# Half-array matmuls for the last token tile and for the last 64 hidden units, another guest batch, and a new place for the transposes of norms

## The chip, the core and the metric

The kernel runs on one core of a Trainium2 chip. Its engines work side by side, each through its own queue in order: TensorE (PE) multiplies matrices into PSUM, VectorE (DVE) and ScalarE (ACT) read PSUM and write SBUF, GpSimd (POOL) works on SBUF and issues some transfers, SyncE (SP) issues the others. The metric is the device time of one execution in microseconds (us). All matmuls are float32; each matmul leaves two records in the trace, each transpose one. "x16" in a row of PE means 16 records.

## The reference, cut to what matters

For each of 16 batches, 100 query tokens of 256 channels attend to 361 context rows of 192 channels with 16 heads of 64 (cross-attention). Then all 1600 tokens pass a mixture of experts: a shared one, and one of seven that a router picks, each a SwiGLU with 704 hidden units.

```python
x = x + xattn(layernorm(x), ctx)         # q = x Wq; k, v = ctx Wkv; softmax(q k / 8) v; Wproj, bproj
h = layernorm(x)
shared = (silu(h @ sw1.T) * (h @ sw3.T)) @ sw2.T
p, e = top1(sigmoid(h @ router_w.T + routing_bias))
w = clip(0.5 + p, 0.5, 2.0)
x = x + 0.5 / w * shared + p / w * expert[e](h)
```

## The kernel before, in words

**Tiles.** The 1600 tokens make 13 tiles of 128; the last (tile 12) has only 64 rows. The 704 hidden units are five chunks of 128 and a rest of 64 (`HALF`). `GROUPS` puts the tiles into groups (0-2), (3-5), (6-8), (9-12).

**Attention.** The main loop walks over 32 steps (b, g): batch b, head half g = 0 or 1. Inside a step, `i` counts four pairs of heads. For each, PE makes the scores (`scores`, L645); DVE takes their maxima (L658), ACT the exponentials (L661); one pair later DVE transposes them (`turning`, L671 and L674). Between the scores PE works through `pairs`, products that other steps need: in (b, 1) the keys of batch b+1 and up to two of its three value products (both L568), in (b, 0) the value product that is left. At the end of a step with g = 0 come, on PE: the `fillers` (projections of finished token tiles, L744, and the router, L240), two query products (L544), and the attention values of batch b-1 (L717), in two halves, one for each of its steps. `moved` (L685 to L705) lies between a step and its L717: SP issues one transfer to `row`, eight to `aT` and two to `over`, POOL eight more to `aT`; then SP loads the context of a later batch (`cT`, L485) and copies guest rows (L587).

PE, ACT, DVE and SP run in the order in which the program is written here (L470). Every matmul product and every transpose takes one of eight PSUM banks in turn (`bank`, L120).

**Norms.** `normalised(g)` queues a group's layer norm in `norms` as parts: moments for each tile, the roots, one `normalise` (L188, DVE) for each tile, and a last part that puts the group's transposes (L208, PE, and the ACT copies to `xT`, L211) into `turns`. `part()` (L778) runs one such part; it is called three times in the loop over `i`, and once or twice behind it. `turns` is emptied at the start of each step with g = 0 (L818 to L820). With `keep`, the transposes also queue the group's router as a filler; its DVE work then goes through `norms` too.

**Guests.** The third key tile of a batch has only 105 of 128 keys, so it leaves 23 columns free. A guest batch has no third value product: five hosts compute its rows in their free columns, and a transfer (`host`, L582) puts them into `w2_sb`, which is not yet in use. Guests are batches 6 and 13, hosts 1 to 5 and 8 to 12.

**Shared expert.** `hidden` (L408) computes the hidden units of a group. The last chunk holds 64 units in its upper half; the lower half of `hT` and of `w2_sb` is set to zero, and `down` (L454) multiplies six chunks of 128 for each tile (L460), six matmuls of 256 columns, adds them into `acc` (L463, DVE) and stores the tile to `base_d`. `project` (L739) does eight matmuls of 256 columns for each tile, for the 64 rows of tile 12 too.

**Experts.** Sorted into tiles by expert, the tokens are gathered from `xn_d` and `base_d`. `turn` (L957) transposes a gathered tile (L960; ACT copies it to `xgT`, L962). A switch on the number of tiles (a load of `e_at`, L1027, and a branch) comes ahead of the loop over expert tiles (L969, L981).

Of the kernel before, what the change touches and what calls it, by code (L numbers as in the profile page):

```python
# [26 lines left out]
P = 128  # L27
# [12 lines left out]
HALF = I - NI * P  # L40
GROUPS = ((0, 1, 2), (3, 4, 5), (6, 7, 8), (9, 10, 11, 12))
FIRST, SECOND = (0, 1), (2, 3, 4, 5)
NS = (N - E) // P + E
NF = (N + P - 1) // P
WE = 2 * 2 * I + (NI + 1) * C
# [1 line left out]


FREE = P - JL
GUESTS = {6: (1, 2, 3, 4, 5), 13: (8, 9, 10, 11, 12)}  # L50
HOSTS = {host: (b, i) for b, hosts in GUESTS.items() for i, host in enumerate(hosts)}
HG = 8
WARM = 6
# [6 lines left out]
def xattn_moe(  # L60
# [18 lines left out]
    def rows(t):  # L79
        return P if t < NT - 1 else LAST  # L80
# [46 lines left out]
        nc.tensor.matmul(nothing[:, :P], ones, ones, start=True, stop=True)  # L127

    nc.gpsimd.memset(acc[LAST:, NT - 1, :], 0.0)
    nc.gpsimd.memset(w2_sb[: P - HALF, NI, :], 0.0)  # L130

    def load_x(g):
        full = [t for t in g if t < NT - 1]
# [85 lines left out]
    def load_shared(i):  # L219

        if i < 4:
            k, o = i // 2, ds(i % 2 * I, I)
            nc.sync.dma_start(w13_sb[:, k, o], w13[ts(k, P), o])
        elif i == 4:
            nc.sync.dma_start(w2_sb[:, :3, :], w2[: 3 * P].rearrange("(i p) c -> p i c", p=P))
        else:
            r = w2[3 * P : NI * P].rearrange("(i p) c -> p i c", p=P)
            nc.sync.dma_start(w2_sb[:, 3:NI, :], r)
            nc.sync.dma_start(w2_sb[P - HALF :, NI, :], w2[NI * P :])

    def router(tiles):

# [175 lines left out]
    def hidden(g, hT, sp, width=NB, same_table=0):  # L408


        n = sum(map(rows, g))

        nc.gpsimd.memset(hT[: P - HALF, NI, :n], 0.0)

        def product(to, at):
            for k in range(2):
                nc.tensor.matmul(  # L417
                    to[:, :n],
                    w13_sb[:, k, ds(at, P)],
                    xT[:, k, ds(g[0] * P, n)],  # L420
                    start=(k == 0),
                    stop=(k == 1),
                )

        def whole(i):
            pa, pb = bank(), bank()
            product(pa, i * P)
            product(pb, I + HALF + i * P)
            s = sp.tile([P, width], F32, name="s")
            if i < same_table:  # L430
                nc.scalar.activation(s[:, :n], pa[:, :n], AF.Tanh, scale=0.5)
                nc.vector.scalar_tensor_tensor(
                    s[:, :n], s[:, :n], 1.0, pa[:, :n], ALU.add, ALU.mult
                )
                nc.vector.scalar_tensor_tensor(
                    hT[:, i, :n], s[:, :n], 0.5, pb[:, :n], ALU.mult, ALU.mult
                )
                return
            nc.scalar.activation(s[:, :n], pa[:, :n], AF.Silu)
            nc.vector.tensor_tensor(hT[:, i, :n], pb[:, :n], s[:, :n], ALU.mult)  # L440

        def rest():

            pa = bank()
            product(pa, NI * P)
            s = sp.tile([P, width], F32, name="s")
            nc.scalar.activation(s[P - HALF :, :n], pa[:HALF, :n], AF.Silu)
            nc.vector.tensor_tensor(
                hT[P - HALF :, NI, :n], pa[P - HALF :, :n], s[P - HALF :, :n], ALU.mult
            )  # L450

        return [lambda i=i: whole(i) for i in range(NI)] + [rest]

    def down(g, hT):  # L454

        for i, t in enumerate(g):
            r = rows(t)
            y = bank()
            for c in range(NI + 1):
                nc.tensor.matmul(  # L460
                    y[:r, :C], hT[:, c, ds(i * P, r)], w2_sb[:, c, :], start=(c == 0), stop=(c == NI)
                )
            nc.vector.scalar_tensor_tensor(  # L463
                acc[:r, t, :], y[:r, :C], coef[:r, t : t + 1], acc[:r, t, :], ALU.mult, ALU.add
            )
            nc.sync.dma_start(base_d[t * P : t * P + r, :], acc[:r, t, :])


    with ExitStack() as attn:
# [10 lines left out]
        def load_ctx(b, parts=1):  # L480
            cT = ap2.tile([P, NR, NJ * P], F32, name="cT")
            of = ctxT[b].rearrange("p (k n) -> p k n", k=NR)
            for i in range(parts):
                k = ts(i, NR // parts)
                nc.sync.dma_start(cT[:, k], of[:, k])  # L485
            return cT

        wq_r = wq.rearrange("p (u k m) -> p u k m", u=NU, k=2)
# [250 lines left out]
        def project(t):  # L739
            r = rows(t)  # L740
            resT = resTs.pop(t)
            pp = bank()
            for c in range(NCH):
                nc.tensor.matmul(  # L744
                    pp[:r, :C], resT[:, c, QP : QP + r], wp_sb[:, c, :], start=(c == 0), stop=(c == NCH - 1)
                )
            nc.vector.tensor_tensor(acc[:r, t, :], pp[:r, :C], acc[:r, t, :], ALU.add)
# [66 lines left out]
        for s, (b, g) in enumerate(steps):  # L814

            if g == 0:  # L818
                while turns:
                    turns.popleft()()  # L820
                pairs = values_of.pop(b)
                if s == 0:
                    ask = lambda: qs.pop(0)() or (lambda: None)
                    pairs[1:] = [ask, ask] + pairs[1:]
                elif (b + 1) % QG == 0 and b + 1 < B:
                    qs = q_units((b + 1) // QG)
            elif b + 1 < B:
# [12 lines left out]
            tb = new_blocks()  # L840
            turning = None
            for i in range(n2):
                exponentials, then = scores(b, g * n2 + i)
                if puts:
                    puts.popleft()()
                exponentials()
                if turning:
                    turning(tb)
                    part()
                turning = then  # L850
                for _ in range(-(-len(pairs) // (n2 - i))):
# [24 lines left out]
        while norms or fillers or turns:  # L876
# [2 lines left out]
                turns.popleft()()  # L879
            if fillers:  # L880
                fillers.popleft()()
        down(GROUPS[0][:2], hT0)
        for at in range(NG):
            values(B - 1, at, *held.pop(0))
        down(GROUPS[0][2:], hT0[:, :, 2 * P :])
        finished(B - 1)
        while fillers:
            fillers.popleft()()
# [28 lines left out]
    def gather_into(to, of, k):  # L917
# [7 lines left out]
            oob_is_err=False,  # L925
        )

    with tc.tile_pool(name="hs", bufs=1) as hs:
        def run_hidden(g):
            n = sum(map(rows, g))  # L930
# [7 lines left out]
            one()  # L938
        hT = run_hidden(GROUPS[1])
        turn_last()  # L940
        down(GROUPS[1][:1], hT)
        for one in router(GROUPS[-1]):
            one()
        down(GROUPS[1][1:], hT[:, :, P:])
        fill = sort_tokens(hs)
        for k in range(NW):
            fetch(k)
# [9 lines left out]
    def turn(k):  # L957
        tr = bank()
        for j in range(2):
            nc.tensor.transpose(tr[:, ts(j, P)], xgs[k % NX][:, ts(j, P)], ident)  # L960
        xgT = xp.tile([P, 2, P], F32, name="xgT")
        nc.scalar.copy(xgT.rearrange("p k n -> p (k n)"), tr[:, : 2 * P])  # L962
        return xgT

    def products(to, xgT, w, units):

# [60 lines left out]
    n = nc.values_load(e_at[:, NS:], min_val=0, max_val=NS - NF)  # L1027
# [63 lines left out]
```

## Time and profile before

| | us |
|---|---|
| median of 3 runs | 721.92 (721.88 to 722.14) |
| the profiled execution | 722.64 |
| its span | 720.9 |
| PE busy in the span | 709.6 |
| DVE busy | 420.4 |
| ACT busy | 280.5 |
| attention, up to the last L645 | about 491 |
| rest of the shared expert, sorting | about 491 to 597 |
| expert tiles | about 597 to 721 |

In a row of the timeline stand the start and the duration in us, the engine, the line, the operation, what it writes and reads, its shape, and the number of records; in brackets the idle time of the engine ahead of it, and what ended it. The mean granted clock of PE is 0.998 of full speed. Ends of matmuls are modelled and overlap with the next start, so that the time of a run of matmuls is best taken from its start to the start of the next.

### The profile page before, as it was taken

How to read it: one execution, taken by the hardware profiler on the slowest of the kernel's cores; microseconds unless marked ns; L12 is line 12 of the kernel's file. 1: busy time of each engine (PE TensorE's matmuls, PEld its weight loads, DVE VectorE, ACT ScalarE, POOL GpSimd, SP SyncE). 2: the span in 40 equal slices, each digit the busy share in tenths (PEclk: the TensorE clock that was granted, in tenths of full speed). 3: DMA queues.
4: the chain of work that ended last, by engine and by line, in shares of the span. 5: the costliest groups of instructions: out<-in, count | busy, mean ns of one | idle time of the engine just before them, and what ended most of it. 6: DMA issues, size and time to landing. Idle time of an engine off the chain costs nothing. (4 is left out here: it accounts for less than half of the span.)

```text
span 720.9 us, 14788 instructions
## 1 busy us (share of the span) xinstructions
PE 709.6 (98%) x5192; PEld 511.7 (71%) x5192; DVE 420.4 (58%) x1090; ACT 280.5 (39%) x791; POOL 198.6 (28%) x419
## 2 busy tenths in 40 slices
PE   9999999999999999999999999999999999999996
PEld 6557657667566766757667676656766588999996
DVE  2777866867787676776777768676247222122121
ACT  2564563534546354463644635543032101111110
POOL 4142322322432222422224222242010103343321
PEclk9999999999999999999999999999999999999999
DMA  7066656454484543636445454465004812898860
GB/s 263 21 143 156 163 143 162 93 144 125 115 214 114 155 118 87 169 89 177 103 113 160 111 146 111 115 160 130 30 30 177 355 37 64 313 347 335 309 248 23
DMA packets 54619, 109.38 MB, mean 152 GB/s; under 512 B 28665, under 2 KB 35964, under 8 KB 52612
## 3 DMA queue, kind: packets, MB, share of 16 engines
q1 hardware_dynamic: 43892, 81.94, 37.1%
q0 software_dynamic: 10352, 25.98, 13.7%
q8 instruction: 44, 0.72, 0.4%
q14 instruction: 43, 0.35, 0.2%
q10 hardware_dynamic: 288, 0.39, 0.2%
HBM read 60.96 MB, written 5.35 MB: 92 GB/s over the span
## 5 line engine op out<-in xcount | busy, mean ns | idle before, releaser
L661 ACT ACTIVATE at<-mm,nm 128x361 f32<-128x361 f32 x256 | 141.7, 559 | 171.4 <-DVE nm L658 171.2
L695 POOL DMA_DIRECT2D aT<-tb x256 | 126.1, 500 | 293.2 <-PE mm L717 100.2
L658 DVE TENSOR_REDUCE nm<-mm 128x1 f32<-128x361 f32 x256 | 123.4, 523 | 60.9 <-PE mm L645 60.0
L674 DVE STREAM_TRANSPOSE tb<-at 128x384 f32<-128x384 f32 x256 | 133.0, 558 | 4.5
L568 PE MATMUL mm<-cT,wk_sb 64*128 64x361 f32 x768 | 125.3, 465 | 1.2 <-DMA wk_sb<-in_wk 0.7
L568 PE MATMUL mm<-wv_sb,cT 64*128 64x512 f32 (+1 forms) x552 | 126.1, 589 | 0.0
L568 PEld LDWEIGHTS mm<-cT,wk_sb 64*128 64x128 f32 x768 | 74.8, 187 | 46.6 <-issue 4.2
L645 PE MATMUL mm<-kT,qT 64*128 64x361 f32 x512 | 97.2, 474 | 0.0
L568 PEld LDWEIGHTS mm<-wv_sb,cT 64*128 64x128 f32 (+1 forms) x552 | 53.2, 185 | 53.6 <-issue 43.4
L969 PE MATMUL mm<-xgT,wex 128*128 128x128 f32 x660 | 78.6, 275 | 0.7 <-ACT xgT L962 0.7
L969 PEld LDWEIGHTS mm<-xgT,wex 128*128 128x128 f32 x660 | 77.0, 192 | 1.8 <-issue 1.1
L717 PE MATMUL mm<-aT,v 128*64 128x100 f32 (+1 forms) x1472 | 72.5, 251 | 1.7 <-DMA over<-row 1.3
L645 PEld LDWEIGHTS mm<-kT,qT 64*128 64x128 f32 x512 | 47.7, 186 | 34.2 <-issue 8.8
L717 PEld LDWEIGHTS mm<-aT,v 128*64 128x64 f32 (+1 forms) x1472 | 67.2, 135 | 6.1 <-issue 3.4
L417 PE MATMUL mm<-xT,w_sb 128*128 128x384 f32 (+1 forms) x176 | 60.9, 503 | 0.0
L417 PEld LDWEIGHTS mm<-xT,w_sb 128*128 128x128 f32 x176 | 32.9, 190 | 26.1 <-issue 8.5
L661 ACT ACTIVATION_READ_ACCUMULATOR at<-mm,nm 128x1 f32 x256 | 50.4, 197 | 0.0
L744 PE MATMUL mm<-wp_sb,resT 128*128 128x256 f32 (+1 forms) x208 | 48.0, 384 | 0.0
L544 PE MATMUL mm<-xT,wq_sb 128*128 128x200 f32 x256 | 46.9, 336 | 0.0
L544 PEld LDWEIGHTS mm<-xT,wq_sb 128*128 128x128 f32 x256 | 43.4, 190 | 4.0 <-issue 1.5
L744 PEld LDWEIGHTS mm<-wp_sb,resT 128*128 128x128 f32 (+1 forms) x208 | 37.8, 186 | 11.2 <-issue 4.4
L608 ACT COPY kT<-mm 128x361 f32<-128x361 f32 x64 | 29.3, 460 | 39.5 <-PE mm L568 39.5
(143 smaller groups left out, 561.2 us busy)
## 6 DMA issues: line engine op xcount, KB each, us to landing
wex<-in_wex SPq DMA_DIRECT2D x15, 2176.0 KB
aT<-tb POOLq DMA_DIRECT2D x256, 80.2 KB, 3.1
aT<-tb SPq DMA_DIRECT2D x256, 80.2 KB
cT<-in_ctxT SPq DMA_DIRECT2D x15, 576.0 KB
over<-row SPq DMA_DIRECT2D x64, 100.0 KB
xn_d<-xn SPq DMA_DIRECT2D x12, 128.0 KB
base_d<-acc SPq DMA_DIRECT2D x12, 128.0 KB
w_sb<-in_w SPq DMA_DIRECT2D x4, 352.0 KB
```

The source lines that it names most:

```text
L417: nc.tensor.matmul(to[:, :n], w13_sb[:, k, ds(at, P)], xT[:, k, ds(g[0] * P, n)], start=(k == 0), stop=(k == 1),)
L544: nc.tensor.matmul(pq[:, o, :], wq_sb[:, u, k, ts(o, P)], xT[:, k, ts(g, QG * LQ)], start=(k == 0), stop=(k == 1),)
L568: nc.tensor.matmul(to[o][:height, :width], *operands(o, k), start=(k == 0), stop=(k == NR - 1),)
L608: nc.scalar.copy(kT[:, c, :], to[0][:, :LKV])
L645: nc.tensor.matmul(sc[o][:, :LKV], qTs[b // QG][r, c, ts(b % QG, QB), :], kTs[b][c // 4][r, c % 4, :], start=True, stop=True,)
L658: nc.vector.tensor_reduce(nm[:, o : o + 1], sc[o][:, :LKV], AX.X, ALU.max, negate=True)
L661: nc.scalar.activation(at[:, o, :LKV], sc[o][:, :LKV], AF.Exp, bias=nm[:, o : o + 1], accum_out=sums[:, o : o + 1],)
L674: nc.vector.transpose(tb[:, :, :, o, i * QR : i * QR + 32].rearrange("p j k n -> p k j n"), at[:, o, :].rearrange("p (k j n) -> p k j n", ...
L695: queue.dma_start(aT[ts(j, 32), i].rearrange("p k o n -> p (k o n)"), tb[ts(i, 32), j].rearrange("p k o n -> p (k o n)"),)
L717: nc.tensor.matmul(av[ts(o, DK), i, :], v[:n, ds((2 * c + o) * DK, DK)], aT[:n, :, j, o, ts(i, QR)], start=(j == 0), stop=(j == NJ - 1),)
L744: nc.tensor.matmul(pp[:r, :C], resT[:, c, QP : QP + r], wp_sb[:, c, :], start=(c == 0), stop=(c == NCH - 1))
L969: nc.tensor.matmul(to[:, ts(o, P)], w[:, ds(j * 2 * I + u, P)], xgT[:, j, :], start=(j == 0), stop=(j == 1),)
```

## The change

Six edits in one:

1. `down` now takes pairs of tiles. The last 64 hidden units of one tile of a pair stay in the upper half of the partitions, those of its partner (`LOWER`) are written to the lower half, and the two matmuls of 64 rows are issued one after the other, on the two halves of the array. `w2_sb` holds its last 64 rows in both halves (one more transfer, no memset). Tiles 2, 3 and 12 stay single, with zeros in the lower half. `hidden` writes the last chunk in up to three pieces.
2. `two_halves`: for tile 12, with 64 rows, one half of the chunks goes to the left columns of the array and PSUM partitions 0 to 63, the other half to the right columns and partitions 64 to 127, in turn. ACT copies the upper half into `bp_sb`, DVE adds both. It serves `project` and `down`.
3. Guest 6 with hosts 1 to 5 becomes guest 7 with hosts 2 to 6.
4. For batches that are not hosts, `cT` is loaded with 361 columns for each of its three parts, no longer 384.
5. `turns` is emptied in the loop over `i`, behind the products, in steps with g = 0.
6. The shared expert's last products are ordered (6, 7), 12, (9, 10), (8, 11); the first expert tile is transposed ahead of the last pair.

```diff
+PAIRS = ((0, 1), (5, 4), (6, 7), (9, 10), (8, 11))
+LOWER = tuple(b for _, b in PAIRS)
+SINGLE = tuple(t for t in range(NT) if not any(t in p for p in PAIRS))
...
-GUESTS = {6: (1, 2, 3, 4, 5), 13: (8, 9, 10, 11, 12)}
+GUESTS = {7: (2, 3, 4, 5, 6), 13: (8, 9, 10, 11, 12)}
...
-    nc.gpsimd.memset(w2_sb[: P - HALF, NI, :], 0.0)
...
-            nc.sync.dma_start(w2_sb[P - HALF :, NI, :], w2[NI * P :])
+            for o in range(2):
+                nc.sync.dma_start(w2_sb[ts(o, HALF), NI, :], w2[NI * P :])
...
+    def two_halves(y, products):
+        n = len(products) // 2
+        for i in range(n):
+            for o in range(2):
+                nc.tensor.matmul(
+                    y[ts(o, LAST), :C], *products[o * n + i], start=(i == 0), stop=(i == n - 1)
+                )
+        high = bp_sb[:LAST]
+        nc.scalar.copy(high, y[LAST:, :C])
+        return high
+
+    def down(tiles):
+        ys = [bank() for _ in tiles]
+        for (t, hT, i), y in zip(tiles, ys):
+            if rows(t) == LAST:
+                of = [(hT[:, c, ds(i * P, LAST)], w2_sb[:, c, :]) for c in range(NI + 1)]
+                high = two_halves(y, of)
+                continue
+            for c in range(NI + (len(tiles) == 1)):
+                last = len(tiles) == 1 and c == NI
+                nc.tensor.matmul(
+                    y[:, :C], hT[:, c, ts(i, P)], w2_sb[:, c, :], start=(c == 0), stop=last
+                )
+        if len(tiles) == 2:
+            for (t, hT, i), y in zip(tiles, ys):
+                r = slice(0, HALF) if t in LOWER else slice(P - HALF, P)
+                nc.tensor.matmul(
+                    y[:, :C], hT[r, NI, ts(i, P)], w2_sb[r, NI, :], start=False, stop=True
+                )
...
-                nc.sync.dma_start(cT[:, k], of[:, k])
+                n = NJ * P if b in HOSTS else LKV
+                nc.sync.dma_start(cT[:, k, :n], of[:, k, :n])
...
+            if r == LAST:
+                of = [(resT[:, c, QP : QP + r], wp_sb[:, c, :]) for c in range(NCH)]
+                for one in (pp, two_halves(pp, of)):
+                    nc.vector.tensor_tensor(acc[:r, t, :], one[:r, :C], acc[:r, t, :], ALU.add)
+                return
...
             if g == 0:
-                while turns:
-                    turns.popleft()()
                 pairs = values_of.pop(b)
...
                 for _ in range(-(-len(pairs) // (n2 - i))):
                     product(pairs)
+                while g == 0 and turns:
+                    turns.popleft()()
...
-        down(GROUPS[2], hT2)
-        down(GROUPS[3], hT3)
+        down([(6, hT2, 0), (7, hT2, 1)])
+        down([(12, hT3, 3)])
+        down([(9, hT3, 0), (10, hT3, 1)])
+        ahead = turn(0)
+        down([(8, hT2, 2), (11, hT3, 2)])
...
-    first = turn(0), None
+    first = ahead, None
```

More of the change, by code (lines that the diff above doesn't have):

```diff
@@ L411, in hidden @@
         n = sum(map(rows, g))
-        nc.gpsimd.memset(hT[: P - HALF, NI, :n], 0.0)
+        for t in g:
+            if t in SINGLE:
+                nc.gpsimd.memset(hT[: P - HALF, NI, ds((t - g[0]) * P, rows(t))], 0.0)
         def product(to, at):
@@ L447, in rest @@
             nc.scalar.activation(s[P - HALF :, :n], pa[:HALF, :n], AF.Silu)
-            nc.vector.tensor_tensor(
-                hT[P - HALF :, NI, :n], pa[P - HALF :, :n], s[P - HALF :, :n], ALU.mult
-            )
-        return [lambda i=i: whole(i) for i in range(NI)] + [rest]
-    def down(g, hT):
-        for i, t in enumerate(g):
+            at = 0
+            while at < len(g):
+                to = at + 1
+                while to < len(g) and (g[to] in LOWER) == (g[at] in LOWER):
+                    to += 1
+                of = slice(at * P, min(to * P, n))
+                r = slice(0, HALF) if g[at] in LOWER else slice(P - HALF, P)
+                nc.vector.tensor_tensor(
+                    hT[r, NI, of], pa[P - HALF :, of], s[P - HALF :, of], ALU.mult
+                )
+                at = to
@@ new lines, in hidden @@
+        return [lambda i=i: whole(i) for i in range(NI)] + [rest]
+    def two_halves(y, products):
[25 more added lines that the diff above has]
+                    y[:, :C], hT[r, NI, ts(i, P)], w2_sb[r, NI, :], start=False, stop=True
+                )
+        for (t, _, _), y in zip(tiles, ys):
@@ L457, in down @@
             r = rows(t)
[L458 to L461, printed above, removed]
-                )
-            nc.vector.scalar_tensor_tensor(
-                acc[:r, t, :], y[:r, :C], coef[:r, t : t + 1], acc[:r, t, :], ALU.mult, ALU.add
-            )
+            for of in (y, high) if r == LAST else (y,):
+                nc.vector.scalar_tensor_tensor(
+                    acc[:r, t, :], of[:r, :C], coef[:r, t : t + 1], acc[:r, t, :], ALU.mult, ALU.add
+                )
@@ L881, in xattn_moe @@
                 fillers.popleft()()
-        down(GROUPS[0][:2], hT0)
+        down([(0, hT0, 0), (1, hT0, 1)])
         for at in range(NG):
             values(B - 1, at, *held.pop(0))
-        down(GROUPS[0][2:], hT0[:, :, 2 * P :])
+        down([(2, hT0, 2)])
         finished(B - 1)
@@ L926, in gather_into, with turn @@
         )
+    def turn(k):
+        tr = bank()
+        for j in range(2):
+            nc.tensor.transpose(tr[:, ts(j, P)], xgs[k % NX][:, ts(j, P)], ident)
+        xgT = xp.tile([P, 2, P], F32, name="xgT")
+        nc.scalar.copy(xgT.rearrange("p k n -> p (k n)"), tr[:, : 2 * P])
+        return xgT
     with tc.tile_pool(name="hs", bufs=1) as hs:
@@ L940, in xattn_moe @@
         turn_last()
-        down(GROUPS[1][:1], hT)
+        down([(3, hT, 0)])
         for one in router(GROUPS[-1]):
             one()
-        down(GROUPS[1][1:], hT[:, :, P:])
+        down([(5, hT, 2), (4, hT, 1)])
         fill = sort_tokens(hs)
@@ L952, in xattn_moe @@
         hT3 = run_hidden(GROUPS[3])
-        down(GROUPS[2], hT2)
-        down(GROUPS[3], hT3)
-    hp = ctx.enter_context(tc.tile_pool(name="hp", bufs=2))
[L957 to L963, printed above, removed]
+        down([(6, hT2, 0), (7, hT2, 1)])
[3 more added lines that the diff above has]
+        down([(8, hT2, 2), (11, hT3, 2)])
+    hp = ctx.enter_context(tc.tile_pool(name="hp", bufs=2))
     def products(to, xgT, w, units):
```

## The prediction

> **What bounds the kernel now.** I read the page first, then the timeline of TensorE (PE) around each place that the change touches, then VectorE (DVE) at the same times.
>
> ```profile
> PE 709.6 (98%) x5192; PEld 511.7 (71%) x5192; DVE 420.4 (58%) x1090; ACT 280.5 (39%) x791; POOL 198.6 (28%) x419
> ```
>
> Of a span of 720.9 us PE is busy 709.6, so a time saved or added in its stream counts in full, unless PE then meets a wait. Its waits before were few. The longest two are here, in batch 6:
>
> ```profile
> 204.86 2.35 PE L717 MATMUL mm<-aT,v 128*64 128x100 f32 x48 [1.26 <-DMA over<-row]
> ...
> 208.55 3.91 PE L568 MATMUL mm<-cT,wk_sb 64*128 64x361 f32 x24 [0.53 <-DMA cT<-in_ctxT]
> ```
>
> Below I subtract starts, not ends, since matmuls overlap. L717's 96 records took 5.88 us here against 4.45 elsewhere, and the scores before L568 took 1.41 against 0.71: 2.1 us lost. Batch 6 is the guest and has no projection, so PE outran DVE, and the transfers to `aT` came late. Two more batches show when that bites: the second half of L717 cannot start before about 9.45 us after DVE's last L674 of the previous step (ends 195.39, half starts 204.86; in batch 2, 75.38 and about 84.9). That covers eight issues on SP (5.0 us), the landing, and some 0.8 us of semaphore reads.
>
> Next, batch 10, where the transposes of group 1 go: PE, then DVE.
>
> ```profile
> 321.63 1.99 PE L645 MATMUL mm<-kT,qT 64*128 64x361 f32 x12
> 323.56 3.72 PE L744 MATMUL mm<-wp_sb,resT 128*128 128x256 f32 x16
> ```
> ```profile
> 322.44 0.97 DVE L658 TENSOR_REDUCE nm<-mm 128x1 f32<-128x361 f32 x2 [1.73 <-PE mm L645]
> 323.33 0.16 DVE L671 RECIPROCAL at<-sums 128x2 f32<-128x2 f32 x1
> 323.52 1.04 DVE L674 STREAM_TRANSPOSE tb<-at 128x384 f32<-128x384 f32 x2
> 324.49 0.37 DVE L188 TENSOR_SCALAR xn<-acc,mv,rstd 128x256 f32<-128x256 f32 x1
> 324.77 0.97 DVE L658 TENSOR_REDUCE nm<-mm 128x1 f32<-128x361 f32 x2
> 325.66 0.15 DVE L671 RECIPROCAL at<-sums 128x2 f32<-128x2 f32 x1
> 325.85 1.04 DVE L674 STREAM_TRANSPOSE tb<-at 128x384 f32<-128x384 f32 x2
> 326.81 0.37 DVE L188 TENSOR_SCALAR xn<-acc,mv,rstd 128x256 f32<-128x256 f32 x1
> ```
>
> PE finishes the last scores of the step at 323.56; the last norm of the group (`xn`, L188) is ready at 327.18. Today these transposes stand a batch later, and only PSUM banks could hold them. In the changed order they stand between these two PE lines.
>
> **The moved transposes.** The diff looks as if they only slip behind the first product of a step. But `turns` is now emptied inside the loop, and `part()`, in the same loop, fills it. So a group that gets full at i=2 or 3 of a first step is turned in that very step. The built order confirms it: in batches 6 and 7 the transposes (8 and 6) stand ahead of the last scores, in 10 and 14 (6 each) after them, just ahead of the projection, and their matmuls now carry waits on DVE. Only batches 1 and 5 get the small shift.
>
> Batches 10 and 14: the first four of six transposes need the second norm (324.86), the last two the third (327.18); a transpose is 0.11. So the projection starts at 327.18 + 0.1 + 0.22 = 327.5 instead of 323.56: 3.95, of it 0.65 transposes and 3.3 idle. In 14 the same rows stand at 442.53 and 446.15: 3.95 again. Behind it PE holds projection, router, queries and values; ACT's copies to `xT` go between two exponentials, free. The router's 0.47 and two switches of PE's mode (0.20) come along: +4.6 per batch here.
>
> What is given back a batch later? In batch 11 the step loses its transposes and router; from the last scores of step (10,1) to the second half of L717 it took 14.9. PE alone would need 13.45. But the router's DVE operations now fall into (10,1), 0.6 of them ahead of its last L674 (ended 350.15, 3.98 after those scores began), so 3.98 + 0.6 + 9.45 = 14.1 decides: given back 0.8. Batch 10/11: +3.8.
>
> In batch 15 there is no projection and there are no queries:
>
> ```profile
> 473.10 1.38 PE L645 MATMUL mm<-kT,qT 64*128 64x361 f32 x8
> 474.41 0.54 PE L240 MATMUL mm<-xT,rw_sb 128*32 128x96 f32 x16
> 475.28 4.78 PE L717 MATMUL mm<-aT,v 128*64 128x100 f32 x96 [0.34 <-DMA aT<-tb]
> ```
>
> From the scores at 463.30 to the second half took 14.4. PE would now need 12.4, but the last L674 (4.06 after those scores) goes back by 0.9, since DVE has no slack there: 4.06 + 0.9 + 9.45 = 14.4. Nothing is given back: **+4.6** (down to +3.0 if those 0.9 find room and the transfers land early).
>
> Batches 6 to 8, with the new guest. The guest's saved value product moves from step (5,1) to (6,1), so (5,1) is long again; with eight transposes more in (6,0), PE reaches the second half of L717 about 12.7 after the step begins, the transfers allow 10.95: the 1.43 and 0.78 of batch 6 go. In their place, the last norm in (6,0) and in (7,0) is ready 6.45 after the step begins (as in batch 10, i=1; in 7 DVE trails as it did in 6 before), PE is there at about 5.15: idle 1.4 and 1.65. `cT` of batch 7 is now three runs of 1444 bytes, not one of 4608; it is due 15.7 after the step begins and lands at about 14.7: taken as nothing, at most +0.5. Moved work: transposes +1.07 in 6; in 7 −1.25 +0.85, router +0.67; in 8 −1.67. Sum with the waits: −2.27 + 3.05 − 0.33 = **+0.45**. Batch 7 itself has a projection and a router, so its values do not wait.
>
> Batch 1, whose eight transposes begin at 45.20:
>
> ```profile
> 46.65 0.44 PE L208 MATMUL mm<-ident,xn 128*128 128x128 f32 x2 [0.57 <-DVE xn L188]
> ```
>
> Here the shift does what the diff suggests: behind scores and values the norm (46.59) is ready. 1.81 becomes 0.97: **−0.84**. Batch 5 had no wait: 0.
>
> The clock, a rule against the change: the Trainium skill, "TensorE: Matmul & The Clock Gate", Part 1, says that PE's clock falls to half after an idle window of about 3.4 us. By the rows, the 1.26 us pause at 203.6 left the granted clock at 1.00, and the two pauses of 3.3 fall into 1.4 and 2.1 with matmuls between; no pause of 2.1 is in this trace. By the rule, each could add an estimated 1.7 (half of one window); by the rows 0. I take 0 and keep +3.4 as the upper end.
>
> **The halves.**
>
> ```profile
> 498.11 3.62 PE L744 MATMUL mm<-wp_sb,resT 128*128 128x256 f32 x16
> ...
> 513.97 7.21 PE L744 MATMUL mm<-wp_sb,resT 128*128 128x256 f32 x32
> ```
>
> A record of 256 columns costs 0.216 (16 in 3.45), also in the 64-row tile. Two halves that run together cost as one: L568's 64-row products (12 of 512 columns in 2.57, 0.215 each instead of about 0.43) and L717's 64-column ones (96 of 100 columns in 4.4) show both kinds at nearly twofold. So: five pairs save a matmul of 0.43 each, 2.16; the last tile's projection 8 x 0.216 = 1.73; its down product 6 x 0.216 = 1.30; together 5.19. The skill's "TensorEngine Tiling (Array Packing)", Key Properties, warns that a change of mode drains the array, without a price. The rows price it: L645 takes 0.71 after a full-array matmul and 0.61 after a half one, L568 0.10 more before a full one. The last tile paid two switches already (7.15 against 2 x 3.45). New are 1 in the first pair, 2 in the second, 5 in the run of the last six products: 8 x 0.105 = 0.84. By the row **−4.35**, without the price −5.19; with no overlap, +0.84.
>
> DVE's extra pieces of `hT` and second sums, ACT's copies of 0.37, and SP's second piece of `w2` (0.39) are hidden: the norms of the last group end at 526.9 and are turned at 535.4; the sort's matmuls wait for nothing, as DVE has one sum less ahead of `onehot` there. GpSimd's gather of `base_d` starts some 1.7 later; its first reader had 4.5 to spare, the next gather of `xn_d` about 2.
>
> **The first expert tile's transposes** look like a saved wait:
>
> ```profile
> 597.33 0.44 PE L960 MATMUL mm<-ident,xg 128*128 128x128 f32 x2
> 598.50 0.68 PE L969 MATMUL mm<-xgT,wex 128*128 128x128 f32 x4 [0.74 <-ACT xgT L962]
> ```
> ```profile
> L1027 PEldq TENSOR_LOAD <-e_at x1: 624/624/624, 593.2 to 593.2; - x1
> ```
> ```profile
> L1087 PEldq COMPARE_BRANCH  x2: 326/2051/3776, 594.3 to 711.3; - x2
> ```
>
> But PE's branch took 3.78 from 594.35, until 598.12; L969 had to wait for it anyway. The load ahead of it ran about 17.6 matmuls before PE's own end, and its whole chain is 5.2. Now the last of those 17.6 are short halves, so the lead shrinks from 3.8 to 3.6, and the 0.22 of transposes stands ahead of it: **+0.4** (−0.95 if the branch hides).
>
> **Sum:** −4.35 + 0.4 − 0.84 + 0.45 + 3.8 + 4.6 = +4.1. The profiled execution's 722.64 (its span and 1.74 around it) becomes 726.7; the median, 721.92, lies 0.72 below that execution, so 726.0.
>
> **Rivals.** *The norms are ready in time (faster):* the idle 1.4 + 1.65 + 3.3 + 3.3 in batches 6, 7, 10 and 14 is absent; 4.1 − 9.65 gives 716.4. It decides if L188 ends 3.3 us sooner against PE. For it: DVE idles 1.73 just before. Against: that idling ends with PE's own second scores, and the chain is in order. 0.11. *The halves do not overlap:* 4.1 + 5.2 gives 731.2. Against it: L568 and L717. 0.06. *The waits are partly paid back* (transfers land sooner in 11 and 15, or the branch hides): 722.5. 0.08. The main case, 0.75, has 723.6 to 728.2 for itself.
>
> About 0.2% (1.4 us) is what a measurement can tell from no change. The range 721.8 to 728.8 leaves out the first two rivals. Faster 0.11, within 0.2% 0.07, slower 0.82.
>
> **What would show it.** Right: PE idle on DVE L188 of about 3.3 before L744 in batches 10 and 14, 1.5 in 6 and 7; none at L717 in batch 6, about 2 in 15; the two projections at 513.97 in about 5.4, not 7.15; the first L969 still about 1.5 after the last down product. Wrong: L188 waits under 0.5, or L717 in batch 15 starting two us earlier than the transfers allow here.

## The result, and the profile after

The changed kernel takes 730.87 us (median of five runs, 729.53 to 732.54), the kernel before 721.88 (721.33 to 722.14) beside it: ratio 1.0126, interval 1.0113 to 1.0138. That is +9.0 us where the forecast had +4.1; 730.87 lies above the range of 721.8 to 728.8. The profiled execution took 731.18 with a span of 729.5, so the traces can be subtracted: 729.46 − 720.91 = +8.55 from first to last instruction.

Line numbers are those of each run's own kernel. In the changed one L688 makes the scores, L192 the norms, L212 their transposes, L792 the projection, L760 the attention values, L493 and L499 the down products (whole and half), L475 those of `two_halves`.

The page after: the row of PE, and the granted clock in 40 slices of 18.2 us.

```profile
PE 710.3 (97%) x5192; PEld 512.2 (70%) x5192; DVE 421.7 (58%) x1100; ACT 280.7 (38%) x793; POOL 197.9 (27%) x417
...
PEclk9999999999999999998999999999999999999999
```

PE's busy time hardly moved; the span grew by 8.6, so the loss is not more work: it is idle time, and work done more slowly. The single 8 in PEclk is batch 10; the page before has none. PE in batch 10 after the change:

```profile
322.50 0.78 PE L688 MATMUL mm<-kT,qT 64*128 64x361 f32 x4
323.21 0.44 PE L212 MATMUL mm<-ident,xn 128*128 128x128 f32 x2
324.56 0.44 PE L212 MATMUL mm<-ident,xn 128*128 128x128 f32 x2 [0.92 <-DVE xn L192]
326.98 0.66 PE L212 MATMUL mm<-ident,xn 128*128 128x128 f32 x2 [1.98 <-DVE xn L192]
327.43 6.40 PE L792 MATMUL mm<-wp_sb,resT 128*128 128x256 f32 x16
333.76 0.46 PE L245 MATMUL mm<-xT,rw_sb 128*32 128x96 f32 x12
```

In batch 14, and the last transposes of the norms in batches 6 and 7:

```profile
452.98 5.09 PE L792 MATMUL mm<-wp_sb,resT 128*128 128x256 f32 x16
457.99 0.54 PE L245 MATMUL mm<-xT,rw_sb 128*32 128x96 f32 x16
...
201.25 0.44 PE L212 MATMUL mm<-ident,xn 128*128 128x128 f32 x2 [1.34 <-DVE xn L192]
228.74 0.41 PE L212 MATMUL mm<-ident,xn 128*128 128x128 f32 x2 [1.43 <-DVE xn L192]
```

The waits on the norms (L192) stand where the forecast put them, .92 + 1.98 idle; from the first transpose to the projection it is 4.22 (forecast 3.95), in batch 14 also 4.22. But the projection behind them, 16 records, took 6.33 from start to start, where batch 10 took 3.65 before; in batch 14, 5.02. The table of windows (stretches of the run; length, then busy us of PE, PEld, DVE, ACT, POOL with counts, then PEclk, DMA share, GB/s) says why:

```profile
322.82:326.23 3.41, 1.26 (x8) 0.40 (x4) 3.34 (x10) 2.28 (x8) 0.88 (x2) 1.00 0.87 243
326.23:329.65 3.42, 2.67 (x8) 2.25 (x9) 2.60 (x7) 1.96 (x7) 0.00 (x0) 0.50 0.73 114
449.11:452.53 3.42, 0.53 (x4) 0.24 (x3) 3.39 (x10) 1.55 (x6) 0.14 (x1) 1.00 0.77 226
452.53:455.94 3.41, 3.41 (x9) 2.81 (x10) 1.84 (x5) 1.95 (x6) 0.00 (x0) 0.50 0.67 174
486.67:490.08 3.41, 1.58 (x36) 1.38 (x32) 3.34 (x9) 1.74 (x7) 0.00 (x0) 1.00 0.89 170
...
199.86:203.28 3.42, 2.08 (x12) 1.36 (x12) 3.39 (x9) 2.04 (x7) 1.88 (x3) 1.00 0.99 222
```

After stretches in which PE worked 1.26 or .53 of 3.41 us the granted clock was .50 for the next window in batch 14 and for two in batch 10. The last row is batch 6: its pause of 1.34 left PE 2.08 of work, and nothing fell. Batch 15's pause, the other one of 2 us, left the clock alone this time:

```profile
485.90 2.35 PE L760 MATMUL mm<-aT,v 128*64 128x100 f32 x48
490.29 2.35 PE L760 MATMUL mm<-aT,v 128*64 128x100 f32 x48 [2.04 <-DMA over<-row]
```

The halves, and the end of the shared experts:

```profile
526.32 3.62 PE L792 MATMUL mm<-wp_sb,resT 128*128 128x256 f32 x16
529.87 1.95 PE L475 MATMUL mm<-wp_sb,resT 128*64 128x256 f32 x16
```
```profile
600.51 0.70 PE L499 MATMUL mm<-w_sb,hT 64*128 64x256 f32 x4
601.14 0.44 PE L979 MATMUL mm<-ident,xg 128*128 128x128 f32 x2
601.41 4.48 PE L493 MATMUL mm<-w_sb,hT 128*128 128x256 f32 x20
605.83 0.70 PE L499 MATMUL mm<-w_sb,hT 64*128 64x256 f32 x4
607.94 1.24 PE L1020 MATMUL mm<-xgT,wex 128*128 128x128 f32 x9 [1.41 <-DVE acc L505]
```
```profile
L1138 PEldq COMPARE_BRANCH  x2: 326/2021/3716, 603.8 to 719.8; - x2
```

Tile 12's projection takes 1.88 (529.87 to 531.75) where a whole one takes 3.55: its two halves do overlap. A pair's last matmuls (L499) take .63 together. The first expert product still waits 1.41; the row names L505, but PE's branch ran from 603.84 for 3.72, until 607.56, so by its times it is the branch that ended last; that is read from the times alone.

### The profile page after: what moved, and what is told of

Same layout as the page of the kernel before. It is cut to its first block, busy times and chain, and to the rows that moved or that the text cites. A ratio compares the mean times of both kernels' runs of the same rounds, so it can differ in the third digit from the quotient of the medians.

```text
span 729.5 us, 14805 instructions
## 1 busy us (share of the span) xinstructions
PE 710.3 (97%) x5192; PEld 512.2 (70%) x5192; DVE 421.7 (58%) x1100; ACT 280.7 (38%) x793; POOL 197.9 (27%) x417
## 5 line engine op out<-in xcount | busy, mean ns | idle before, releaser
L688 PE MATMUL mm<-kT,qT 64*128 64x361 f32 x512 | 97.4, 473 | 0.0
L760 PE MATMUL mm<-aT,v 128*64 128x100 f32 (+1 forms) x1472 | 72.2, 251 | 2.0 <-DMA over<-row 2.0
L688 PEld LDWEIGHTS mm<-kT,qT 64*128 64x128 f32 x512 | 48.4, 186 | 34.5 <-issue 9.7
L760 PEld LDWEIGHTS mm<-aT,v 128*64 128x64 f32 (+1 forms) x1472 | 67.1, 135 | 6.6 <-issue 5.2
L792 PE MATMUL mm<-wp_sb,resT 128*128 128x256 f32 x192 | 48.5, 410 | 0.0
L792 PEld LDWEIGHTS mm<-wp_sb,resT 128*128 128x128 f32 x192 | 38.9, 207 | 10.0 <-issue 2.5
```

The source lines that it names most:

```text
L688: nc.tensor.matmul(sc[o][:, :LKV], qTs[b // QG][r, c, ts(b % QG, QB), :], kTs[b][c // 4][r, c % 4, :], start=True, stop=True,)
L760: nc.tensor.matmul(av[ts(o, DK), i, :], v[:n, ds((2 * c + o) * DK, DK)], aT[:n, :, j, o, ts(i, QR)], start=(j == 0), stop=(j == NJ - 1),)
L792: nc.tensor.matmul(pp[:r, :C], resT[:, c, QP : QP + r], wp_sb[:, c, :], start=(c == 0), stop=(c == NCH - 1))
```

## The experiments

Ratios are to the kernel before on the same chip (720.3 to 722.0 there). A step is meant by (batch, g), and its start is that of its first scores in the trace.

**Transposes early again** (the change without its moved transposes):

```
             if g == 0:
+                while turns:
+                    turns.popleft()()
...
-                while g == 0 and turns:
-                    turns.popleft()()
```

> The changed kernel with the transposes of norms back at the start of a step; everything else stays. Theory (the moved transposes cost their waits for norms, and in batches 10 and 14 some 4 us of half clock on top): 715.5 us, from 721.9 - 3.2 (halves and branch, as the trace after shows from 480 to L1020) - 2.2 (the two waits of batch 6) - 0.4 to 1.3 (start, and a fetch pause among the experts that the trace after does not have). No pause over 1 us on L188, clock 1.0 throughout. Rival (the other edits make it slower, the moved transposes are only where it shows): over 725.

716.5 us, ratio .9937 (.9921 to .9954). Everything but the moved transposes gains; they alone cost some 14. PE in batch 10 then:

```profile
320.18 1.99 PE L688 MATMUL mm<-kT,qT 64*128 64x361 f32 x12
322.10 3.72 PE L792 MATMUL mm<-wp_sb,resT 128*128 128x256 f32 x16
```

The projection follows the scores at once, at full clock. The expectation of 715.5 started from 721.9; this chip's kernel before took 720.71, so the gain is 4.2 instead of 6.4. Between the two traces the halves and the branch gave 3.07 for the 3.2 expected (118.51 to 115.44, from step (15,1) to the first expert product). The shortfall in the traces is in batches 6 to 8: from (1,1) to (8,1) 212.02 against 213.05, a gain of 1.03 for the 2.2 that the two waits of batch 6 were to give.

**The moved transposes alone** (the same lines, put into the kernel before):

> The kernel before with nothing but the moved transposes. Theory: 734 us, from 721.9 - 0.8 (batch 1) + 0.5 (batches 6 to 8, where guest 6 loses its waits to the norms) + 6.2 (10 and 11) + 6.3 (14 and 15), with half clock for 3.4 or 6.8 us behind each of the two long pauses. Rival: under 726, the clock falls only together with the half-array matmuls.

736.02, ratio 1.0200 (1.0177 to 1.0222): +15.3, expected +12.1 for two drops of the clock. The clock fell at four places, after batches 6, 10, 14 and 15; in batch 15 behind this pause:

```profile
487.44 2.35 PE L717 MATMUL mm<-aT,v 128*64 128x100 f32 x48
491.88 3.48 PE L717 MATMUL mm<-aT,v 128*64 128x100 f32 x47 [2.09 <-DMA over<-row]
```

The second half took 3.48 instead of 2.35. In the changed kernel the same wait of 2.04 cost nothing more. So a pause of 2 us sometimes costs the clock, and sometimes not. The rival falls: the clock drops without any half-array matmul of the change.

**The pause filled** (the changed kernel with 12 matmuls of ones, whose result nobody reads, ahead of the transposes):

```
                while g == 0 and turns:
+                    if b in (10, 14):
+                        busy = bank()
+                        for _ in range(12):
+                            nc.tensor.matmul(busy[:, :P], ones, ones, start=True, stop=True)
                    turns.popleft()()
```

> The changed kernel with 12 matmuls of ones (128x128) ahead of the transposes in batches 10 and 14, some 2.7 us of work for nothing in pauses of 3.3 us; the result is not touched. Theory (an idle window halves PE's clock for one or two windows of 3.4 us): clock 1.0 throughout, the projections of 10 and 14 in 3.65 instead of 6.3 and 5.0, 726.8 us. Rival (these projections are slow because DVE, ACT or PSUM banks hold them): 731 or more, projections as slow as in the changed kernel.

727.58, ratio 1.0089 (1.0072 to 1.0106), although PE does more. Batch 10:

```profile
323.36 2.94 PE L903 MATMUL mm<-ones 128*128 128x128 f32 x24
326.14 0.60 PE L212 MATMUL mm<-ident,xn 128*128 128x128 f32 x4
327.13 0.41 PE L212 MATMUL mm<-ident,xn 128*128 128x128 f32 x2 [0.39 <-DVE xn L192]
327.38 3.62 PE L792 MATMUL mm<-wp_sb,resT 128*128 128x256 f32 x16
```

The norms come no sooner, but the projection takes 3.62 again: steps (10,0) and (14,0) take 20.49 each, not 23.47 and 22.18. In this profile the clock fell in batch 15 instead, where step (15,0) took 15.87, not 14.35; the time stayed above the expected 726.8. By the four runs, that is the clock: the two with a mean granted clock of .999 and 1.000 took 727.18 and 726.19, the two with .997 took 727.98 and 728.28. The rival (DVE, ACT or the banks hold the projections) falls: with the clock kept they take 3.62, and DVE, ACT and the banks are as before.

**All pauses filled** (as before, and 12 more in batch 15 ahead of the second half of the value products):

```
                for at in range(NG):
+                    if b == 15 and at == 1:
+                        busy = bank()
+                        for _ in range(12):
+                            nc.tensor.matmul(busy[:, :P], ones, ones, start=True, stop=True)
                    values(b - 1, at, *held.pop(0))
```

> The changed kernel with 12 matmuls of ones ahead of the transposes in batches 10 and 14, as in the earlier run with the pauses filled, and 12 more in batch 15 ahead of the second half of its value products, where that run lost its clock instead. Theory, that the clock alone is what my sum lacked: no half clock in the attention, the pauses are only covered and no wait is gone, so the time is the changed kernel's 730.9 less the 4.05 us by which the two projections were slowed: 726.5 to 727, near my forecast of 726.0. Rival, that the fills shorten a wait elsewhere or that the clock falls again at another place: 727.6 or above, as in the earlier run.

728.01, ratio 1.0081 (1.0067 to 1.0095). By its time this is a miss: it lies on the rival's side. Its trace shows no half clock, and from step (0,0) to (15,0) it took 458.14 us against 462.17 in the changed kernel, −4.03 (the theory: 4.05). Steps (10,0) and (14,0) got shorter by 2.98 and 1.70. What came back:

```profile
482.41 2.35 PE L760 MATMUL mm<-aT,v 128*64 128x100 f32 x48
484.69 2.94 PE L920 MATMUL mm<-ones 128*128 128x128 f32 x24
487.56 2.35 PE L760 MATMUL mm<-aT,v 128*64 128x100 f32 x48
```

No wait is left in batch 15: the 2.87 of ones are longer than the wait, and step (15,0) takes 15.11 instead of 14.35, +.76. The rest is a later start (16.60 against 16.06) and .60 in the experts' stretch, both of which also vary between kernels that are alike there (starts from 15.68 to 16.93). So the trace shows the cause; the median alone would not.

**Pauses of TensorE by themselves** (40 bursts in front of the kernel; GpSimd cannot write before the burst has read, nor the next burst start before it has written):

```
+    for _ in range(5):
+        for length in (800, 1000, 1250, 1500, 1700, 1950, 2400, 3100):
+            for _ in range(64):
+                nc.tensor.matmul(nothing[:, :P], ones, row[:, :P], start=True, stop=True)
+            nc.gpsimd.memset(row[:, :length], 0.0)
```

> A measurement of the clock by itself: the kernel with the transposes early and whole context loads, with a stretch in front of it of 40 bursts of 64 matmuls, each followed by a pause of TensorE while GpSimd fills 800 to 3100 elements a partition (about 0.9 to 3 us, five pauses of each length). In the traces so far every change of the granted clock lies on a grid of 3.413 us, and a stretch of the grid in which TensorE stood idle for .475 of it or more was followed by one at half clock (with one exception at .534), and none with .419 or less. Theory, that this share decides: pauses under 1.5 us never drop the clock, pauses of 1.7 to 2.1 about half of the time, according to how they lie on the grid, pauses of 3 nearly always. Rival, that the length of a pause decides: each length always or never. Second rival, the rule that I kept as the upper end with no weight (a whole window of idle time): none of these pauses drops it.

A single profiled run of 1376.1 us, that stretch included. The pauses are .88 to 2.89 long; six dropped the clock: two of five of 1.90, two of five of 2.27, two of five of 2.86 to 2.89. Where a run has more than one drop, all begin on one grid, that is, whole multiples of 3.413 us apart; the grid lies elsewhere in each run. Three windows of that grid, each with the one behind it:

```profile
97.73:101.15 3.42, 1.52 (x14) 1.33 (x13) 0.00 (x0) 0.00 (x0) 1.72 (x1) 1.00 0.00 0
101.15:104.56 3.41, 3.41 (x19) 3.41 (x18) 0.00 (x0) 0.00 (x0) 0.00 (x0) 0.50 0.00 0
131.87:135.28 3.41, 1.52 (x14) 1.32 (x12) 0.00 (x0) 0.00 (x0) 1.77 (x1) 1.00 0.00 0
135.28:138.70 3.42, 2.46 (x22) 2.46 (x23) 0.00 (x0) 0.00 (x0) 0.91 (x1) 1.00 0.00 0
527.81:531.23 3.42, 1.49 (x13) 1.49 (x14) 0.00 (x0) 0.00 (x0) 1.88 (x1) 1.00 0.00 0
531.23:534.64 3.41, 3.41 (x19) 3.41 (x18) 0.00 (x0) 0.00 (x0) 0.00 (x0) 0.50 0.00 0
```

The first two pairs show the same 1.52 of work; their pauses are 1.900 and 1.892 long within the window. A pause that put 1.89 us or less into one window never dropped the clock (34 of 34), one that put 1.90 or more into one always did (6 of 6). A pause of 1.90 that the grid cut into .68 and 1.22 was free, and one of 2.86 cut into 1.89 and .96 too. Both rivals fall: length alone does not decide, and no whole window is needed. My shares were a little off: pauses of 3 dropped it twice in five, not nearly always. In the attention the border seems to lie elsewhere: there windows with 1.79 (the transposes alone, batch 6) and 1.67 (only behind the first pair, batch 7) of work were followed by half clock, and batch 15's with 1.58 in the changed kernel was not.

```profile
195.78:199.19 3.41, 1.79 (x14) 0.92 (x10) 3.35 (x9) 1.85 (x7) 3.39 (x7) 1.00 0.87 222
225.08:228.49 3.41, 1.67 (x12) 0.92 (x10) 3.38 (x9) 1.11 (x5) 1.38 (x3) 1.00 0.34 101
```

The modelled ends may explain this: a record's shown end lies past the point where the next could start, so every break in a window adds work that was not done. An estimate without them counts each record from its start for .84 ns a column (.216 us for 256 columns). These two windows then hold 1.32 each, and batch 15's holds 1.43. Of all windows at full clock with less than 2.4 us of shown work, in all traces, those with 1.34 or less of work so counted were followed by half clock, those with 1.41 or more were not. The one exception is the window at 131.87, with 1.31. This count was made after the runs and no run tests it.

**Only behind the first pair of a step** (the loop emptied at `i == 0` alone):

```
-                while g == 0 and turns:
+                while g == 0 and i == 0 and turns:
```

> The changed kernel with the transposes taken from the queue behind the first product of a step only (i = 0), so that no group is turned in the step in which its last norm is made. Theory: 714.7 us, e1's 715.5 less the 0.8 of batch 1. No wait on L188 over 0.5 us. Rival (a place behind the first scores is itself costly, for the exponentials or the banks): above e1.

720.16, ratio .9983 (.9976 to .9991): a miss by 5.5. The waits on norms were gone, but in batch 7 another took their place:

```profile
224.44 1.09 PE L212 MATMUL mm<-ident,xn 128*128 128x128 f32 x8
225.46 0.88 PE L688 MATMUL mm<-kT,qT 64*128 64x361 f32 x4
228.08 2.40 PE L688 MATMUL mm<-kT,qT 64*128 64x361 f32 x7 [1.74 <-ACT at L704]
```

The eight transposes took two PSUM banks between two pairs of scores, the next scores waited 1.74 for ACT to free banks, and the clock fell behind that from 228.49. Its twenty runs show what this drop is worth: seven with a mean granted clock of .998 or .999 took 718.2 to 719.5, thirteen with .996 or .997 took 719.3 to 720.8. Even the best of them is 3.5 above the expected 714.7. Steps (6,1) and (7,0) took 34.39 together in the trace, with the transposes early 30.54.

**The halves alone** (edits 1 and 2 in the kernel before, with the order of the last products from edit 6; the rest as before):

> The kernel before with edits 1 and 2 alone (pairs and two halves; the first expert tile's transposes stay at the end, the guest and the context loads are as before, the transposes of the norms ahead of the scores). By the durations of the changed kernel: pair (0, 1) -0.23, pair (5, 4) -0.14, the last two groups -1.7, the projection of tile 12 -1.72, in all -3.8 us: 716.9 beside a run of 720.7. The forecast had -4.35, and with the pieces of .63 instead of .53 us nothing else should differ. Rival, halves that don't overlap: +0.8, 721.5. Second rival, that the end is set by the routing (the branch) and not by TensorE: the last products end earlier but the first expert product does not, about -1.7 and 719.0.

717.4, ratio .9952 (.9940 to .9964): −3.4, expected −3.8, forecast −4.35. The end of the shared experts:

```profile
586.71 0.70 PE L499 MATMUL mm<-w_sb,hT 64*128 64x256 f32 x4
587.35 4.58 PE L493 MATMUL mm<-w_sb,hT 128*128 128x256 f32 x20
591.86 0.70 PE L499 MATMUL mm<-w_sb,hT 64*128 64x256 f32 x4
592.49 0.44 PE L978 MATMUL mm<-ident,xg 128*128 128x128 f32 x2
593.64 1.58 PE L1018 MATMUL mm<-xgT,wex 128*128 128x128 f32 x12 [0.71 <-DVE acc L505]
```

From step (15,1) to the first expert product it took 114.87, before 118.51: −3.64. Two matmuls in the two row halves take .64 (586.71 to 587.35) where one whole matmul takes .43.

**The guest alone** (7 with hosts 2 to 6 in the kernel before):

```
-    GUESTS = {6: (1, 2, 3, 4, 5), ...}
+    GUESTS = {7: (2, 3, 4, 5, 6), ...}
```

> The kernel before with edit 4 alone: batch 7 as the guest in place of 6, full context loads, transposes ahead of the scores. From the run with the transposes early (everything but the moved transposes), the stretch from the start of batch 0 to the second step of batch 8 was 255.09 us long, before 256.14: -1.05 us, of which none comes from the halves. So 719.7 beside 720.7. If the trimmed context loads were behind that, and not the guest, this run shows 720.7. If the swap costs what the forecast wrote for batches 6 to 8 (+0.45, with the transposes behind), 721.2.

720.0, ratio .9986 (.9978 to .9995). From step (0,0) to (8,1) 255.17 against 256.14: −.97, as expected. With the transposes early the new guest saves 1.0. With them late, the stretch took 258.00 in the run of the transposes alone (old guest) and 256.19 in the changed kernel (new guest); these 1.81 are about the cost of the one window at half clock behind batch 6, which only the run with the old guest has. So a saving by the swap itself is not shown there.

**The first expert tile's transposes at the end, and whole context loads** (each undone in the kernel with the transposes early; the two ran on one chip):

```
-        ahead = turn(0)
...
-    first = ahead, None
+    first = turn(0), None
```

> The kernel with the transposes early, with the first expert tile's two transposes put back to their place behind the last pair. The wait at the branch was 1.48 us there and .27 us for the transposes is no longer hidden in front of it, but before, with the transposes behind the branch's start, the wait was 1.18. Theory, [...] the transposes fill part of the wait, -0.3 to -0.6 us, 716.0 beside 716.5. Rival, that the transposes ahead of the last pair save their whole .65 us: +0.65, 717.1.

```
-                n = NJ * P if b in HOSTS else LKV
-                nc.sync.dma_start(cT[:, k, :n], of[:, k, :n])
+                nc.sync.dma_start(cT[:, k], of[:, k])
```

> The kernel with the transposes early, with whole context loads (one contiguous row for a partition instead of three pieces of 1444 bytes) as before. The wait of .754 us for batch 7's context should go if the three pieces made the load late: -0.75, 715.75. Rival, that the wait comes from where the load is issued with the new guest: no change, 716.5. The later start of .46 us that the other run with trimmed loads also showed (16.54 against 16.08) says that the start doesn't hang on the load's form.

716.64 (ratio .9940) and 716.29 (.9939): by their times nothing between them. By the traces, the stretch from (15,1) to the first expert product is 114.67 to 114.94 long in the four kernels with halves and the turn at the end, and 114.99 to 115.44 in the seven with it ahead: about +.3 for the turn ahead, in traces whose two ranges hardly part. Batch 7's wait for its context, with the trimmed load and then with the whole one:

```profile
209.70 2.70 PE L611 MATMUL mm<-cT,wk_sb 64*128 64x361 f32 x16 [0.75 <-DMA cT<-in_ctxT]
```
```profile
209.17 3.27 PE L610 MATMUL mm<-cT,wk_sb 64*128 64x361 f32 x19 [0.31 <-DMA cT<-in_ctxT]
```

It shrinks by .44, it does not go; the run of the guest alone, with whole loads, waits .55 there, so the form of the load is at most a part of it. In the changed kernel PE comes later and has no such wait.

**Batch 1 alone.** The first try kept `while turns` at the step's start for all batches but 1, and the loop behind the pairs as the change has it:

> Everything of the change that paid, and nothing else: halves, the new guest, whole context loads, the transposes of the norms behind the scores in batch 1 alone (ahead of them in every other batch), the first expert tile's transposes at the end. From 716.64 with the transposes early and the turn at the end: whole context -0.45, batch 1 -0.8, together 715.4 beside a run before of 720.8. It also tells whether the loss of the run in which only the first pair of scores kept its place (+3.85 from batch 7's second pair and the half clock behind it) came from batch 7 alone: if batch 1's transposes were part of it, this run is at 717 or above, and its granted clock falls in the middle of the attention.

730.49, ratio 1.0135 (1.0112 to 1.0157). The kernel was not what I meant: that loop still emptied the groups that got full within a step, in every batch. So it is the changed kernel with the turn at the end and whole loads, it lost the same 9 to 10 us with the same drops, and it says nothing of batch 1. It does show where the fault lies: not in a later start, but in a loop that stays open. With it open in batch 1 alone:

```
+                while b == 1 and g == 0 and turns:
```

> The run before this one that was to move batch 1's transposes alone left the loop behind the pairs open in every batch, so it was the changed kernel without the turn ahead and the trimmed loads (730.5 against 730.9), and says nothing of batch 1. Here that loop empties the transposes in batch 1 alone. 716.64 with the transposes early and the turn at the end, whole context -0.45, batch 1 -0.8: 715.4 beside a run before of 720.7, and no pause above 1.7 us and no half clock in the attention. Rival: batch 1's transposes behind the scores are themselves what the run with only the first pair moved lost by: 717 or above.

715.83, ratio .9919 (.9906 to .9933), the lowest ratio of all, and no half clock before the end. Batch 1:

```profile
48.57 1.09 PE L212 MATMUL mm<-ident,xn 128*128 128x128 f32 x8
49.59 0.57 PE L687 MATMUL mm<-kT,qT 64*128 64x361 f32 x2
```

Eight transposes without a wait; from (0,0) to (1,1) 42.30, with the turn at the end and the transposes early 43.10: −.80. The expected ratio, 715.4 to 720.7, was .9926: met, within the interval.

## Why the prediction was wrong

The sign and the mechanism of the main loss were right; the sum was too small. Step by step, differences of starts in the two profiled executions:

| stretch | forecast | measured |
|---|---|---|
| batch 1, (0,0) to (1,1) | −.84 | −.79 |
| batches 6 to 8, (1,1) to (8,1) | +.45 | +.84 |
| batches 10/11, (10,0) to (12,0) | +3.8 | +6.57 |
| batches 14/15, (14,0) to (15,1) | +4.6 | +6.36 |
| halves and the turn, (15,1) to the first expert product | −3.95 | −3.14 |
| start and expert tiles | 0 | −.43, −.89 |

**The step that failed is the clock:** "by the rows 0. I take 0 and keep +3.4 as the upper end". The two projections were slowed by 2.68 and 1.37, 4.05 in all. That is most of what the sum lacked: 4.45 in all, 5.8 without the last row of the table, whose stretches vary by themselves. Filling the pauses took 4.03 off up to step (15,0), while the projections began only .2 sooner (9.12 after the start of their step, before 9.32); that shows the cause. The upper end itself was too low: I allowed half a window for each, and in batch 10 the clock stayed at half for two. My reason for 0 was that the pauses come in pieces with matmuls between. The Trainium skill, "TensorE: Matmul & The Clock Gate", Part 1, says that the window is free-running and 3413 ns long, which the traces confirm; I read its "idle window" as one that is idle throughout. The pauses by themselves show that 1.90 us of idle time in one window is enough, and that pieces add up is shown in batch 10: its window from 322.82 held .92 and, before the grid cut the second pause at 326.23, 1.23.

**The waits on the norms** were right: 4.22 for 3.95 in 10 and in 14, 1.34 and 1.43 for 1.4 and 1.65 in 6 and 7; batch 6's wait at L760 is gone, batch 15's is 2.04. The two projections of the last group took 5.43 together (5.4 forecast), and the first expert product began 1.48 after the last down product (1.5). Without the clock's 4.05, batches 10/11 cost 3.89 (forecast 3.8) and 14/15 cost 4.99 (4.6). "Nothing given back" in batch 15 held.

**The halves** gave about 3.65 (the run of them alone), not 4.35: the term mis-sized is the price of the mode, "8 x 0.105 = 0.84". The two matmuls in row halves take .63 to .64 where I had .43 for the pair and .1 for a switch. Over five pieces that is .5 of the missing .7; the rest is not traced. The projection was right (−1.67 measured as 3.55 − 1.88, forecast −1.73).

**The first expert tile's transposes** cost about .3, forecast .4; by its times the branch ended last, as forecast.

**Batches 6 to 8** cost .4 more than forecast, and two terms of that sum were off in opposite ways. The two waits of batch 6 were to give 2.27 back (a slip: the rows shown give 1.43 + .70 = 2.13), and the swap with the transposes early gave 1.0. The moved transposes were to cost 3.05 − .33 = 2.72 there and cost 1.87 (213.89 against 212.02 with them early). How the two depend on each other isn't settled: with the transposes early batch 7 waits for its context, with them late it does not. The start, and a pause in the expert tiles (.93 in the tile at 615.22 before, absent after; an expectation calls it a fetch pause, but its cause is not shown), vary between kernels that are alike there, so −1.3 of the measured +8.55 is not the change's.

## What to carry to other kernels

When a change adds a wait of TensorE, count the idle time that can fall into any one window of the clock (3.413 us here), pieces together: from about 1.6 to 1.9 us of shown idle time on (the least that dropped it here, in the attention and in the bursts), add one to two windows at half speed as a likely cost. If the wait can't go, fill the pause with matmuls whose result nobody reads. When work is taken from a queue that the same loop fills, look for the items that get full in that very pass: "behind the first product" became "as soon as it is ready, and often before". The version that keeps such a move to the batch where the wait was (here batch 1) beat both kernels.

## What the runs showed of the hardware

- The granted clock changes on a grid of 3.413 us. Between bursts of full-array matmuls it fell to half behind each window with 1.90 us or more of idle time (6 of 6) and behind none with 1.89 or less (34 pauses). A window of half speed behind a burst cost 1.63 us there (16.19 against 14.56 for the burst).
- Whether such a pause costs depends on where the grid lies, which differs from run to run: a pause of 1.90 was free where the grid cut it and dropped the clock where it did not. The changed kernel's five times spread over 3.0 us, from 729.53 at a mean granted clock of .994 to 732.54 at .990; those of the kernel before, on the same chip, over .8.
- Once down, the clock stayed at half for a second window where PE had little to do in the first (2.67, 2.22 and 2.29 us of shown work, in three traces); behind windows with 3.25 or more it was full again (16 of 16).
- Two matmuls in the two row halves of the array take 1.5 times one whole matmul (.63 to .43). A projection in two column halves takes 1.06 times half of a whole one (1.88 to 1.78).
